# A graph kernel's rounds: rows of 133 edges with five self-loops taken out, and the loops added per chunk

## The chip, the cores and the metric

The kernel runs on one core of a Trainium2 chip. The metric is the device time of one execution in microseconds (us): the median of 10 runs is 10170.87 us, between 10168.81 and 10172.67. The engines go by short names: PE is TensorE, DVE is VectorE, ACT is ScalarE, POOL is GpSimd and SP is SyncE. SP, ACT and POOL also issue DMAs; gathers by index are issued by POOL.

## The reference

Two graph layers on 20000 nodes with 256 features and 340000 edges. The edges are 160000 random pairs, taken in both directions, and one self-loop for each node; they are sorted by destination with a stable sort, so a node's own loop is the last of its edges. Every edge, a loop too, has a type from 0 to 7. The first layer is relational: each type has a weight matrix of its own, and it is applied twice.

```python
def _rgcn_layer(x, W, self_w, b, src, dst, edge_type, num_nodes):
    xW = jnp.einsum('ni,rio->rno', x, W)
    msg = xW[edge_type, src]
    agg = jax.ops.segment_sum(msg, dst, num_segments=num_nodes)
    return agg + x @ self_w + b
...
h = jax.nn.relu(_rgcn_layer(x, W1, self_w1, b1, src, dst, edge_type, N_NODES))
out = _rgcn_layer(h, W2, self_w2, b2, src, dst, edge_type, N_NODES)
...
x = _layernorm(x + out)
```

The second layer is an attention over the same edges with 4 heads, in which source and destination are exchanged (it sums over all edges of equal source), followed by another layer norm. Everything is float32.

## The kernel before

The kernel has three stages: round one and round two (the two applications of the relational layer, `round_one` and `round_two`, both through `by_chunks`), and `attention`. A last branch recomputes everything in a general way if a flag (`bad`) says that an assumption about the edges does not hold.

**Tiles and chunks.** The sorted edges are cut into tiles of 128 (2657 of them, `COLS`); 16 tiles (`T`) make a chunk, of which there are 166 (`NC`; the last one has 17 tiles). The destinations of a chunk lie in a frame of 128 nodes that begins at `bases[j]`; those of tile t lie in a fixed window of that frame (`windows`), 16 to 19 nodes wide. All chunks are unrolled.

**What a tile does.** POOL gathers the 128 source rows (`gather`, L643). In the first 28 chunks of round one (`RAW`) a row is x in f32, later it is the row split into three bf16 parts (table `xs` in round one, `h2s` in round two). DVE makes one-hot matrices over (node in the window, type) from a code of each edge (`compare_raw`, L656; `compare`, L666). PE multiplies the gathered rows with the one-hots and adds up in PSUM (L764): for each of two halves of the features, for each part, for each half of the frame (64 nodes x 8 types, one PSUM bank of 512 columns) that the window touches. So a tile is 6 products in bf16, 12 where its window crosses the middle, and each streams 8 times as many columns as the window has nodes. Four banks hold the sums of the two feature halves (h) and the two frame halves (q).

**What a chunk does.** After tile 8 the first half of the frame is copied out of PSUM, after the last tile the second one (`evacuate`; three copies on ACT at L688, one on DVE at L686). The frame's first 12 nodes get what the chunk before left for them (L776). `make` then turns the frame's own rows (L695 or L698, copy `ot` on ACT at L701), multiplies them with the self weights (L707), adds the bias (L709) and multiplies the 8 types' sums with their weights, 16 products in f32 (L711); it yields between them, and one step of it runs after each tile of the next chunk. `use` finishes the rows and writes them to DRAM: `h2s` in round one; in round two a layer norm, a product with the attention's weights (L945, L953) and the tables for attention.

**Order of the work.** Instructions are emitted by hand in this order (`manual_schedule`): for each tile u, the gather of tile u + 23 (`AHEAD`; there are 24 buffers `g`), the comparisons, the tile's products, evacuation, one step of `make`, perhaps one step of side work, and one step of `use`. Each engine executes its share in that order. Side work comes from generators: `heads` (the rest of `edges`, then `fill_rows` and `ends_weights`), then `split_rows` (x into three bf16 parts, table `xs`), then `order`, which sorts the edges by source for attention (`rank` on ACT and DVE, `places`, `write` with the products L1271 on PE and the activations `two` on ACT, and `unpack`). In round one a tile takes a side step always until `rank` begins, then 2 tiles of 3, and 5 of 9 once `placed`; in round two 5 of 9. What is left over of `order` runs after round two; `unpack` has 23 gathers (L1361).

**The head.** `edges` reads source, destination and type in 5 slices of up to 5 x 128 tiles, 128 edges to a partition row, turns them on PE to 128 edges to a column, and makes of them the gather's index (`idx`), the code, and what the ordering needs (`hi`, `lo`, `kb`, `flat`). The index of slice 0 depends on the source's load alone. `load_ends` and `place_frames` compute `bases` from the first, middle and last edge of each chunk.

Of the kernel before, what the change touches and what calls it, by code (L numbers as in the profile page):

```python
# [47 lines left out]
P = 128  # L48
# [7 lines left out]
T = 16  # L56
CH = T * P
T3 = 17

TH = T // 2  # L60
BN = P // 2

HOME = BN - 1
CARRY = 12

AHEAD = 23

QS = 5

LOT = 3  # L70
# [7 lines left out]
def gnn_kernel(  # L78
# [37 lines left out]
    NC = E // CH  # L116

    RAW = min(28, NC // 2)
    COLS = -(-E // P)
    CS = QS * P  # L120
    assert CS % T == 0
    WORDS = NB * (T3 + 1)
    assert WORDS >= COLS
    assert COLS - NC * T in (0, 1)
# [6 lines left out]
    G = P // RG  # L131
    NK = -(-NB // 3)
    assert NB * 171 >> 9 == NB // 3 and NK <= STEP and NK * APART < 2 ** 23
    NQ = -(-COLS // P)
# [3 lines left out]
    slope = N * P / E  # L138
    vary = 3.0 * slope / P ** 0.5
    lows = [max(0, int(HOME + slope * (t - TH) - 3 - 0.35 * vary * abs(t - TH) ** 0.5)) for t in range(T + 1)]  # L140
    ends = [min(P, int(HOME + slope * (t + 1 - TH) + 4.5 + 0.5 * vary * abs(t + 1 - TH) ** 0.5)) for t in range(T)] + [P]
    lows[0], ends[T - 1] = 0, P
# [3 lines left out]
    halves = [(0, TH), (TH, T), (T, T + 1)]  # L146
    widths = [max(b - a for a, b in windows[f:g]) for f, g in halves]
    WIDE = max(P, NB, R * max(widths))
# [22 lines left out]

    slotd = dram.tile([EP, F], I32, name="slotd")
# [198 lines left out]
    def load_ends(pool, fb):  # L371

        ends_of = [pool.tile([1, NC], I32, name=f"ends{i}") if i != 1 else fb[0:1].bitcast(I32) for i in range(3)]
        for i, c in enumerate((0, CH // 2, CH - 1)):
            e = nc.scalar if i == 1 else nc.sync
            e.dma_start(ends_of[i], dst[:NC * CH].rearrange("(j c) -> c j", c=CH)[c:c + 1, :])
        return ends_of

    def place_frames(ends_of, to):
# [4 lines left out]
        nc.vector.tensor_single_scalar(mid, mid, HOME, op=ALU.subtract)  # L384
# [8 lines left out]
    def edges(k, keep, pool, ps, words):  # L393


        full, more = E // P, E % P or P
        if more == P:
            full -= 1
        QF, RF = full // P, full % P
        assert NQ == QF + 1  # L400
        slices = [(q, min(QS, NQ - q)) for q in range(0, NQ, QS)]

        def flat(of, q, n, none, e, after=0):

            c = pool.tile([P, QS, P], I32, name="flat", bufs=4)
            a = min(n, QF - q)
            of = of[after:]
            if a < n:
                nc.vector.memset(c[:, a:n], none)
            if a:  # L410
                e.dma_start(c[:, :a], of[q * P * P:(q + a) * P * P].rearrange("(q r p) -> r q p", r=P, p=P))
            if a < n:
                if RF:
                    e.dma_start(c[:RF, a], of[QF * P * P:full * P].rearrange("(r p) -> r p", p=P))
                if more > after:
                    e.dma_start(c[RF:RF + 1, a, :more - after], of[full * P:].unsqueeze(0))
            return c

        def number(c, n, e):
            f = pool.tile([P, QS, P], F32, name="flatf", bufs=3)  # L420
            e(f[:, :n], c[:, :n])
            return f

        def turned(f, q, n, to, idx=None):

            for i in range(0, n, 4):
                pt = ps.tile([P, 512], F32, name=("pr", "pl")[i // 4 % 2])
                m = min(4, n - i)
                for x in range(m):
                    w = min(P, COLS - (q + i + x) * P)  # L430
                    o = pt[:, x * P:x * P + w]
                    if f.dtype == BF16:
                        nc.tensor.matmul(o, f[:w, i + x, :], identb[:w, :w], start=True, stop=True)
                    else:
                        nc.tensor.transpose(o, f[:w, i + x, :], ident[:w, :w])
                w = min(m * P, COLS - (q + i) * P)
                if idx is not None:
                    nc.vector.tensor_scalar_max(idx[:, i * P:i * P + w], pt[:, :w], 0.0)
                nc.scalar.copy(to[:, i * P:i * P + w], pt[:, :w])
                yield  # L440

        for name, of in zip(("hi", "lo"), words):
            k[name] = of[:, :COLS]
        k["kb"] = keep.tile([P, COLS], FP16, name="kb")
        k["flat"] = keep.tile([P, NQ, P], F32, name="flatv")
        k["idx"], k["code"] = [], []
# [3 lines left out]
        begin = pool.tile([P, T + 1], F32, name="begin")  # L450
        end = pool.tile([P, T + 1], F32, name="end")
        for t, (a, b) in enumerate(windows):
            nc.gpsimd.memset(begin[:, t:t + 1], float(R * a))
            nc.gpsimd.memset(end[:, t:t + 1], float(R * (b - a)))
        q, n = slices[0]
        got = {0: [flat(src, q, n, -P, nc.sync), flat(dst, q, n, -NP, nc.sync), flat(etype, q, n, 0, nc.scalar)]}
        fb = pool.tile([P, NC], F32, name="fb")
        ends_of = load_ends(pool, fb)
        got[0].append(flat(dst, q, n, NP, nc.scalar, 1))
        odd = pool.tile([P, CS], BF16, name="odd")  # L460
        nc.vector.memset(odd, 0.0)
        own = pool.tile([P, CS], BF16, name="ownloops")
        nc.vector.memset(own, 0.0)

        def loads(s):
            return [flat(src, *slices[s], -P, nc.sync), flat(dst, *slices[s], -NP, nc.sync),
                    flat(etype, *slices[s], 0, nc.sync)]

        for s, (q, n) in enumerate(slices):
            fs, fd, ft, after = got.pop(s)  # L470
            c = q * P
            w = min(n * P, COLS - c)
            j = c // T
            m = (min(c + w, NC * T) - c) // T
            rest = w - m * T
            lo, hi = k["lo"][:, c:c + w], k["hi"][:, c:c + w]
            idx = keep.tile([P, w], I32, name=f"idx{s}")
            k["idx"].append(idx)
            block = pool.tile([P, QS, P], I32, name="block", bufs=1)
            if s:  # L480
                nc.vector.tensor_single_scalar(block[:, :n], fs[:, :n], 7, op=ALU.arith_shift_right)
            raw = fs
            fs = number(fs, n, nc.vector.tensor_copy)
            yield from turned(fs, q, n, lo, idx) if s else ()
            if not s:
                for _ in turned(fs, q, n, lo, idx):
                    pass
            fd = number(fd, n, nc.scalar.copy)
            if s:
                yield  # L490
                yield from turned(fd, q, n, hi)
            else:
                for _ in turned(fd, q, n, hi):
                    pass
            ft = number(ft, n, nc.scalar.copy)
            ct = pool.tile([P, CS], BF16, name="ct")
            if s:
                yield
                yield from turned(ft, q, n, ct)
            else:  # L500
                for _ in turned(ft, q, n, ct):
                    pass
                firsts = place_frames(ends_of, k["bases"])
                step = pool.tile([1, 2, NC], F32, name="step")
                ff = step[:, 1]
                nc.vector.tensor_copy(ff, k["bases"])
# [1522 lines left out]
```

## Time and profile before

| what | value |
|---|---|
| median of 10 runs | 10170.87 us |
| the profiled execution | 10177.42 us |
| its span, first to last instruction | 10175.6 us |
| mean granted TensorE clock | 0.957 |
| busy PE / PEld / DVE / ACT / POOL, us | 8655.1 / 6511.3 / 6451.5 / 6353.0 / 7659.7 |
| gathers of round one, first and last start | 7.2 and 3371.9 us |
| gathers of round two, first and last start | 3393.2 and 6720.4 us |
| gathers of attention, first start | 6754.3 us |

Busy time by stage, from the view of busy time by window:

| window, us | PE | DVE | ACT | POOL | clock |
|---|---|---|---|---|---|
| 0 to 590 | 497.9 | 334.6 | 201.1 | 445.1 | 0.96 |
| 590 to 2000 | 1203.0 | 680.5 | 683.1 | 1066.7 | 0.93 |
| 2000 to 3380 | 1210.7 | 719.1 | 644.0 | 1041.6 | 0.95 |
| 3380 to 6200 | 2603.4 | 1478.6 | 1652.3 | 2123.3 | 0.98 |
| 6200 to 6720 | 487.3 | 239.8 | 239.6 | 393.6 | 0.99 |
| 6720 to 10176 | 2652.9 | 2998.9 | 2932.9 | 2589.4 | 0.95 |

In the lines of the profile, L764 is line 764 of the kernel before; `g<-h2s,idx` is a gather that writes g from table h2s by the index; "x2657" counts instructions; then come busy time and the mean length of one, and behind the bar the idle time of the engine ahead of them, with what ended it. PEld is the loading of PE's stationary operand. Products overlap in PE's pipeline, so their lengths are longer than the distance from one start to the next. In the timeline a line has start, length, engine, line, operation, operands and count, and in brackets how long the engine was idle before and who ended that.

### The profile page before, as it was taken

The numbers are of one execution on the slowest core, as the hardware profiler recorded it, in microseconds if no ns is written. First come the engines' busy times: TensorE is split into PE (matmuls) and PEld (weight loads), VectorE is DVE, ScalarE is ACT, GpSimd is POOL, SyncE is SP. The second block draws the span as 40 slices with busy tenths as digits, with TensorE's granted clock in tenths as the row PEclk, the third lists the DMA queues.
The fourth block names the chain that finished last, engine by engine and source line by source line (L and its number), as shares of the span: only waits on it lengthen the run. The fifth ranks groups of instructions, "written<-read, shape, count | busy, mean of one in ns | idle before, by whom it ended". The sixth has DMA issues, their size and how long they took to land. (4 is left out here: it accounts for less than half of the span.)

```text
span 10175.6 us, 197290 instructions
## 1 busy us (share of the span) xinstructions
PE 8655.1 (85%) x67798; PEld 6511.3 (64%) x67798; DVE 6451.5 (63%) x14086; ACT 6353.0 (62%) x18671; POOL 7659.7 (75%) x8045
## 2 busy tenths in 40 slices
PE   8988888888898899999999999977777777777777
PEld 7866667666777777777777777754444444444444
DVE  6532366665444455555555555458888888888888
ACT  2466533332555555555555555538888888888888
POOL 7777777777777677777777777777777777777776
PEclk9999999999999999999999999989999999999999
DMA  5866666665666666666666666655555555555554
GB/s 168 255 204 177 177 178 177 178 178 171 177 179 179 180 189 188 190 189 188 189 188 189 189 189 189 190 157 155 155 154 152 155 155 155 153 154 155 153 154 129
DMA packets 860686, 1776.34 MB, mean 175 GB/s; under 512 B 196943, under 2 KB 526356, under 8 KB 859652
## 3 DMA queue, kind: packets, MB, share of 16 engines
q0 software_dynamic: 461200, 1384.74, 48.7%
q1 hardware_dynamic: 390620, 371.69, 11.5%
q8 instruction: 534, 8.75, 0.3%
q10 hardware_dynamic: 7848, 7.20, 0.2%
q14 instruction: 484, 3.96, 0.1%
HBM read 1629.85 MB, written 133.22 MB: 173 GB/s over the span
## 5 line engine op out<-in xcount | busy, mean ns | idle before, releaser
L764 PE MATMUL a<-s,g 128*128 128x152 bf16 (+9 forms) x34860 | 2870.0, 226 | 418.9 <-DMA g<-xs,idx 322.7
L1453 POOL DMA_INDIRECT g<-table3s,words x2657 | 2566.6, 966 | 813.5 <-issue 780.4
L643 POOL DMA_INDIRECT g<-h2s,idx x2657 | 2517.9, 948 | 830.6 <-issue 372.1
L711 PE MATMUL pm<-wt,to 128*128 128x256 f32 x10624 | 2921.5, 398 | 0.0
L764 PEld LDWEIGHTS <-g 128*128 128x128 bf16 x32844 | 2182.0, 99 | 949.2 <-DMA g<-xs,idx 420.5
L643 POOL DMA_INDIRECT g<-xs,idx x2209 | 2108.3, 954 | 680.6 <-issue 341.2
L1555 ACT ACTIVATE g<-g 128x64 f32<-128x64 f32 x8088 | 1993.1, 332 | 0.0
L711 PEld LDWEIGHTS pm<-wt,to 128*128 128x128 f32 x10624 | 1832.6, 192 | 187.9 <-issue 10.4
L1569 PE MATMUL po<-g,s 128*128 128x260 f32 x5314 | 1737.7, 418 | 96.3 <-DVE g L1561 70.6
L1513 DVE CUSTOM_DVE_ANT_0 dump<-pr,pen 128x768 bf16<-128x768 f32 x1876 | 1619.5, 907 | 30.0 <-PE pr L1510 28.6
L688 ACT COPY to<-a 128x512 f32<-128x512 f32 x996 | 545.1, 582 | 1376.6 <-PE a L764 1355.0
L1510 PE MATMUL pr<-hpt,pick 128*128 128x512 bf16 (+2 forms) x3752 | 936.6, 332 | 421.8 <-DVE top L1513 420.0
L1251 ACT ACTIVATE two<-b,words 128x157 f16<-128x157 f16 x2657 | 1120.6, 422 | 62.8 <-PE pl L1271 51.7
L1569 PEld LDWEIGHTS po<-g,s 128*128 128x128 f32 x5314 | 849.3, 196 | 454.5 <-ACT g L1546 78.3
L1252 ACT ACTIVATE two<-b,words 128x157 f16<-128x157 f16 x2657 | 1104.9, 416 | 0.0
L1510 PEld LDWEIGHTS <-pick 128*128 128x128 bf16 x3752 | 379.7, 101 | 922.3 <-issue 799.4
L776 DVE TENSOR_TENSOR to<-to,to 128x192 f32<-128x192 f32 x330 | 118.9, 360 | 1306.8 <-ACT to L688 1306.8
L666 DVE TENSOR_TENSOR s<-pi,code 128x1216 bf16<-128x1216 f32 x610 | 856.7, 1408 | 1.1 <-PE a L764 1.1
L1271 PE MATMUL pl<-two,a 128*128 128x314 f16 x2657 | 569.6, 303 | 122.4 <-ACT two L1252 118.3
L1013 DVE TENSOR_TENSOR b<-pi,kb 128x471 f16<-128x471 f32 (+1 forms) x896 | 567.9, 634 | 0.0
L1499 ACT CAST hpt<-pr 12x768 bf16<-12x768 f32 (+1 forms) x469 | 350.2, 747 | 344.1 <-PE pr L1497 343.9
L643 POOL DMA_INDIRECT g<-in_x,idx x448 | 440.5, 983 | 138.0 <-issue 67.7
(329 smaller groups left out, 8945.3 us busy)
## 6 DMA issues: line engine op xcount, KB each, us to landing
ob<-ownd SPq DMA_DIRECT2D x625, 128.0 KB
g<-h2s,idx POOLq DMA_INDIRECT x2657
g<-table3s,words POOLq DMA_INDIRECT x2657
g<-xs,idx POOLq DMA_INDIRECT x2209
h2s<-h SPq DMA_DIRECT2D x166, 192.0 KB
own<-h2s SPq DMA_DIRECT2D x166, 192.0 KB
xs<-xs SPq DMA_DIRECT2D x156, 192.0 KB
own<-xs SPq DMA_DIRECT2D x136, 192.0 KB
```

Source lines behind the costliest of these rows:

```text
L643: nc.gpsimd.indirect_dma_start(out=g, out_offset=None, in_=of, in_offset=bass.IndirectOffsetOnAxis(ap=idx[u // CS][:, u % CS:u % CS + 1], ...
L666: nc.vector.tensor_tensor(s, pi[:, :w].unsqueeze(1).to_broadcast([P, e - f, w]), codes(c, e - f).unsqueeze(2).to_broadcast([P, e - f, w]), ...
L711: nc.tensor.matmul(p, to[:, i % 2, i // 2, :P], wt[:, i % 2, i // 2, :], start=False, stop=(i == 2 * R - 1))
L764: nc.tensor.matmul(a[h, q][:, b:e, :].rearrange("p n r -> p (n r)"), g[:, v * D + h * P:v * D + (h + 1) * P], s, start=((h, q) not in begu ...
L1251: nc.scalar.activation(two[:, 0, :], made[m][:, x, :], AF.Copy, scale=k["hi"][:, c:c + 1])
L1252: nc.scalar.activation(two[:, 1, :], made[m][:, x, :], AF.Copy, scale=k["lo"][:, c:c + 1])
L1271: nc.tensor.matmul(pl[0].rearrange("p a b -> p (a b)"), a[:, x, :], ranked.pop((m, x)).rearrange("p a b -> p (a b)"), start=(first and x = ...
L1453: nc.gpsimd.indirect_dma_start(out=g[:, t, :], out_offset=None, in_=table3s, in_offset=bass.IndirectOffsetOnAxis(ap=to3[:, b, t:t + 1], ax ...
L1510: nc.tensor.matmul(pr[:, t:t + n, :], pick[:, h, :], k["hpt"][:, q + t:q + t + n, :], start=True, stop=True)
L1513: nc.vector.tensor_tensor_reduce(out=dump[:, :m, :].rearrange("p t e -> p (t e)"), in0=pr[:, :m, :].rearrange("p t e -> p (t e)"), in1=k[" ...
L1555: nc.scalar.activation(gh[:, h, :], gh[:, h, :], AF.Copy, scale=k["g"][:, t, D + h:D + h + 1])
L1569: nc.tensor.matmul(k["po"], k["s"][:, t, :] if t < n else ident, k["g"][:, t, :SR], start=(t == 0), stop=(t == n))
```

## The change

A row now has 133 edges (`LEN`) instead of 128. Of each row the self-loops among the nodes 0 to 4 after the row's first one, five of them, are taken out; the other 128 edges are pressed together and make a tile. There are 2557 tiles, 15 to a chunk, and 171 chunks (the last has 7 tiles). 120 rows make a block, and slices are two blocks wide. The 75 loops of a chunk are kept apart, with their nodes in the frame and their types; a round trip through DRAM (`loopd`) brings them from rows to columns.

- Index and code of a slice are made by more steps on DVE, with masks and predicated copies; the index now also depends on `bases`.
- For each chunk DVE makes two one-hots of its loops (`loop_marks`, at tile 6 of the chunk before); PE multiplies them to a mask of node and type, and DVE spreads that mask over a half of 64 nodes by 8 types (`loop_hots`, at tile 9).
- At tile 0 (first half of the frame) and at tile 3 (second half) PE multiplies the frame's own rows, 64 of them, with the spread mask (`loop_sums`). These products open the PSUM sums; no product of a tile does any more.
- Windows are 17 to 21 nodes wide instead of 16 to 19; the last tile's extra window is gone. `AHEAD` goes from 23 to 21, `RAW` from 28 to 30 chunks; in round one loop products are in f32 for 32 chunks.
- The side work changes its order: after two slices come `fill_rows` and `split_rows`, then the other slices. Its pace goes from 2 of 3 to 3 of 4 tiles, and from 5 of 9 to 3 of 5. `records` goes away, since `edges` makes `hi` and `lo` itself.

```diff
-T = 16
-CH = T * P
+T = 15
+LEN = P + 5
+DROP = LEN - P
+ROWS = 8 * T
+SLOTS = T * DROP
+CH = T * LEN
...
-AHEAD = 23
-
-QS = 5
+AHEAD = 21
+
+QS = 2
...
-    RAW = min(28, NC // 2)
...
+    RAW = min(30, NC // 2)
...
+            nc.vector.tensor_mul(same, same, over)
+            drop = pool.tile([P, QS, LEN], BF16, name="drop")[z, :n]
+            nc.vector.scalar_tensor_tensor(drop, far, DROP - 0.5, same, op0=ALU.is_lt, op1=ALU.mult)
...
+            nc.vector.tensor_scalar_min(by, far, float(DROP))
+            nc.vector.scalar_tensor_tensor(by, drop, -16.0, by, op0=ALU.mult, op1=ALU.add)
...
+            for x in range(DROP + 1):
...
+                mask = pool.tile([P, QS, P], BF16, name="mask", bufs=2)[z, :n]
+                nc.vector.tensor_single_scalar(mask, by[:, :, x:x + P], float(x), op=ALU.is_equal)
+                nc.vector.copy_predicated(kept, mask.bitcast(I16), v[:, :, x:x + P])
...
+            pt = turned(kept, q, n)
+            vt = pool.tile([P, QS * ROWS], I32, name="vt")[:, :w]
+            nc.scalar.copy(vt, pt)
...
+            nc.vector.tensor_single_scalar(k["idx"][:, c:c + w], vt, 9, op=ALU.arith_shift_right)
...
+            lot = loopd[q * ROWS * DROP:(q + n) * ROWS * DROP]
+            nc.sync.dma_start(lot.rearrange("(q r k) o -> r q (k o)", r=ROWS, k=DROP), loops)
...
+            nc.sync.dma_start(ls, lot.rearrange("(j s) o -> s (j o)", s=SLOTS))
...
+        def loop_marks(j):
...
+            a = sp.tile([SLOTS, P], BF16, name="la")
+            nc.vector.tensor_tensor(a, pi[:SLOTS, :P], k["node"][:, j:j + 1].to_broadcast([SLOTS, P]), op=ALU.is_equal)
+            b = sp.tile([SLOTS, R], BF16, name="lb")
+            nc.vector.tensor_tensor(b, pi[:SLOTS, :R], k["type"][:, j:j + 1].to_broadcast([SLOTS, R]), op=ALU.is_equal)
+            loop[j] = a, b
...
+        def loop_hots(j):
...
+            a, b = loop.pop(j)
+            x = WIDE + 1 + 3 * NK + j % 2 * R
+            po = pi[:, x:x + R]
+            nc.tensor.matmul(po, a, b, start=True, stop=True, skip_group_check=True)
+            s = sp.tile([P, 2 * BN * R], BF16, name="lm", bufs=1)
+            s = s.bitcast(F32) if raw and j < raw + 2 else s[:, :BN * R]
+            loop[j] = s
+            nc.vector.tensor_tensor(s.rearrange("p (n r) -> p n r", r=R), k["half"].unsqueeze(2).to_broadcast([P, BN, R]),
+                                    po.unsqueeze(1).to_broadcast([P, BN, R]), op=ALU.mult)
...
+        def loop_sums(j, q):
+
+            own, s = loaded[j][0], loop[j]
+            x = slice(q * BN, (q + 1) * BN)
+            n_parts = 1 if own.dtype == F32 else 3
+            for h in range(2):
+                a[h, q] = ps.tile([P, BN, R], F32, name=f"a{h}{q}")
+                for v in range(n_parts):
+                    nc.tensor.matmul(a[h, q].rearrange("p n r -> p (n r)"), own[x, v * D + h * P:v * D + (h + 1) * P],
+                                     s[x], start=(v == 0), stop=(v == n_parts - 1), skip_group_check=True)
...
+        while "ready" not in k:
+            next(side)
+        loop_marks(0)
+        loop_hots(0)
...
+            if t == TH - 2:
+                loop_marks(j + 1)
...
+            if t == TH + 1:
+                loop_hots(j + 1)
+            if t in (0, 3):
+                loop_sums(j, t // 3)
...
-                                         start=((h, q) not in begun), stop=(v == n_parts - 1), skip_group_check=True)
-                        begun.add((h, q))
+                                         start=False, stop=(v == n_parts - 1), skip_group_check=True)
...
+        for i, _ in enumerate(parts):
+            yield
+            if i % 2:
+                yield
+        with tc.tile_pool(name="edges", bufs=1) as cp:
+            pools[0] = cp
+            yield from rest
...
-                  lambda u: not ranks.begun or (u % 9 < 5 if ranks.placed else u % 3), False, ranks, RAW, parts)
+                  lambda u: not ranks.begun or (u % 5 < 3 if ranks.placed else u % 4), False, ranks, RAW, parts)
```

## The prediction

> **What bounds the kernel now.** I read the page first: the 40 slices and the costliest groups.
>
> ```profile
> PE   8988888888898899999999999977777777777777
> ...
> POOL 7777777777777677777777777777777777777776
> ...
> L711 PE MATMUL pm<-wt,to 128*128 128x256 f32 x10624 | 2921.5, 398 | 0.0
> ...
> L643 POOL DMA_INDIRECT g<-h2s,idx x2657 | 2517.9, 948 | 830.6 <-issue 372.1 <-PE a L764 231.3 <-PE pl L1271 90.8
> ```
>
> The two rounds fill slices 1 to 26, attention the rest. POOL shows 7 throughout and looks far from full; PE shows 8 in round one and 9 in round two. Which of them sets the pace? The timeline of POOL in round two answers for the gathers:
>
> ```profile
> 5002.18 0.95 POOL L643 DMA_INDIRECT g<-h2s,idx  x1 [0.30 <-PE a L764]
> 5003.43 0.95 POOL L643 DMA_INDIRECT g<-h2s,idx  x1 [0.30 <-PE a L764]
> 5004.69 0.95 POOL L643 DMA_INDIRECT g<-h2s,idx  x1 [0.31 <-PE pl L1271]
> ```
>
> A gather starts every 1.25 us, and the gap is 0.30 us whoever is named as its releaser, "issue" included: POOL never waits longer there, it is simply full at 0.95 + 0.30. So a tile costs POOL 1.25 us and a chunk of 16 tiles 20.0 us. Next, the waits of PE's weight loads and matmuls: first round one from 800 to 2000 us, then round two from 3500 to 6200 us (us in total, times, longest):
>
> ```profile
> PEld L764 <- DMA g<-xs,idx: 225.5, 230, 3.5
> ...
> PEld L764 <- DMA g<-h2s,idx: 11.0, 20, 0.9
> ...
> PE pl L1271 <- ACT two L1252: 85.0, 230, 0.6
> PE pr L1304 <- DVE here L1293: 74.2, 22, 5.9
> ```
>
> In round one PE waits for gathers 225 us in 1200. In round two almost never: there PE is as slow as POOL. To see how near, I counted in the timeline how long after the end of the u-th gather the u-th tile's first product starts:
>
> | tile | 90 | 210 | 450 | 540 | 2400 | 3000 | 3600 | 4200 | 4700 | 5300 |
> |---|---|---|---|---|---|---|---|---|---|---|
> | lag, us | 20.7 | 4.3 | 19.8 | 5.7 | 2.2 | 11.2 | 17.0 | 23.6 | 26.0 | 2.3 |
>
> (Tiles from 2657 on are round two.) While round two carries the ordering's products (L1271), the lag climbs to 26 us, which is all 23 gathers of AHEAD. **PE needs about 20.2 us a chunk there, 0.15 more than POOL, and is the bound already**; buffers hide it. Where it catches up, it shows its own speed: tiles 90 to 210 in 137.9 us, 18.4 us a chunk (raw, f32 products); tiles 450 to 540 in 99.2 us, 17.6 a chunk, of which 1.5 are waits for ACT (ot, L701) behind the copies of the row split.
>
> **What the change does to each.** Prices are start to start, from PE's timeline:
>
> ```profile
> 3379.04 7.17 PE L711 MATMUL pm<-wt,to 128*128 128x256 f32 x32
> 3386.05 0.70 PE L1271 MATMUL pl<-two,a 128*128 128x314 f16 x4
> ...
> 5011.20 1.35 PE L764 MATMUL a<-s,g 128*128 128x152 bf16 x18
> 5012.38 0.56 PE L1271 MATMUL pl<-two,a 128*128 128x314 f16 x3
> ...
> 7503.06 0.48 PE L1510 MATMUL pr<-hpt,pick 128*128 128x512 bf16 x2
> 7503.38 0.60 PE L1569 MATMUL po<-g,s 128*128 128x260 f32 x2
> ```
>
> 18 products of 152 columns take 1.18 us: 0.43 ns a column. The L1510 pair is one product of 512 and one of 256 columns: 0.32 us for 768, so 0.21 us for 512. An f32 product is two records; 32 records of 256 columns take 7.01 us, 0.219 each, so an f32 product of 512 columns costs 4 x 0.219 = 0.88 us. 128 active rows or 1 active column make no visible difference in the rows; the columns streamed do.
>
> *Removed.* 100 tiles a round (2657 to 2557): 200 gathers x 1.25 = 250 us of POOL. A chunk falls to 15 tiles, 18.8 us of POOL.
>
> *Added on PE, per chunk.* loop_sums: 2 halves x 2 feature halves x 3 bf16 parts = 12 products of 512 columns, 12 x 0.215 = 2.58 us. While own rows come in f32 (32 chunks): 4 x 0.88 = 3.5 us. loop_hots: one product of 8 columns, under 0.05. Windows widen: their sum is 285 nodes over 16 tiles before, 296 over 15 after, so a chunk streams 296 x 8 x 6 columns instead of 285 x 8 x 6: 528 x 0.43 = +0.23 us. The make (32 L711 records and the rest) stays the same per chunk, and there are 171 chunks instead of 166, which the sums below include. Net +2.83 us a chunk (+3.8 raw) against 1.25 us less time on POOL.
>
> *Where that lies.* PE is in order, and loop_sums stands in its stream at tiles 0 and 3. Its operands are early: own rows are loaded two chunks ahead, the marks are made at tiles 6 to 9 of the chunk before; its PSUM was evacuated at tile 8 and at the last tile, about 4 us before tile 3 needs it. So I give it no wait, but no cover either: nothing hides 2.8 us on an engine that is the bound.
>
> *DVE and ACT.* loop_marks and loop_hots add three DVE instructions, about 0.3 + 0.2 + 0.7 us (nearest rows: L1258, 384 wide, 0.55; L686, 512 wide, 0.69). DVE is busy 1479 of 2820 us in round two; covered. If that cover went, 1.2 us a chunk would be 400 us. The edge slices' DVE steps (266 instead of 640 wide, more of them) run beside gathers as before. SP gets 11 stores and 11 loads of loops and five more chunks' rows; it is not near full. The row split moves ahead of the later slices, with its 157 loads and 157 stores on SP and two ACT copies each; that removes POOL's 7.8 us wait for xs, worth nothing once PE is the bound.
>
> *Head.* Now the first gather starts at 7.2 us and the first product at 19.9. After, the index needs the frames (ends landed at 7.9, then 8 small DVE instructions and nine tiny products), some 15 DVE instructions of 266 columns at about 0.35 (640-wide ones take 0.49 to 0.82), twelve masks and predicated copies at 0.3, a turn and two copies: first gather about 24 us. The first chunk also waits for the loops: 16 more instructions and reductions, a store and a load through DRAM (the first load here is issued at 0.8 and used at 4.2 us), marks: first product about 46 us. POOL loses 17 us, PE 26.
>
> **The sum, along PE.** In the built program's order the ordering's products span chunks 137 to 331 of 342 (123 to 322 of 332 before).
> - raw, 32 chunks: 18.4 + 3.8 = 22.2 us, 710
> - chunks 32 to 136, 105: 17.6 - 1.5 (split done earlier) + 2.8 = 18.9; POOL asks 18.8; with friction 19.2: 2016
> - 34 chunks of round one with L1271: 18.9 + 13.3 x 0.133 + waits for "two" 0.5 = 21.2: 721
> - 22 us between rounds, as now
> - round two, 160 chunks: 20.2 + 2.8 = 23.0 if every wait stays. The idle of PE before L1271 and L1304 is 159 us over 134 chunks, 1.2 us each; longer PE time gives ACT and DVE more room, so I take half of it as hidden: 22.4, 3584
> - 11 chunks without L1271: 19.9, 219
>
> 46 + 710 + 2016 + 721 + 22 + 3584 + 219 = 7318 us, where round two now ends at 6722: +596. The 23 gathers of unpack (29 us on POOL after round two) fall into PE's backlog: -25. Attention (3450 us) is untouched. The profiled execution took 10177.4 us (span 10175.6), so 10748; the median of the runs is 6.5 us below the profiled one: **about 10740 us, 5.6% slower**.
>
> **The Trainium skill.** "TensorE: Matmul & The Clock Gate", section "Why this matters for your kernels", says that a matmul of few contraction rows takes as long as a full one and gains only from tiles running side by side. The half-row loop products stand three tiles apart in the stream, so by it nothing is saved; no row here has 64 rows. The same page's "Back-to-back issue gap" gives 131 ns for sustained 512-column matmuls; the 0.215 us above differ, and the measurement decides. By its figure 3720 products would cost 312 us less, and the time would be about 10430.
>
> **Rivals.**
> 1. *POOL stays the pace* (faster). If half-row products cost little, under about 0.05 us, and PE's waits melt, the time is 10171 - 250 + 17 = about 9940. For it: PE's busy time holds pipelined tails. Against: at the prices above, without any wait or tail, PE's products of round two sum to 17.4 us a chunk now (L764 5.9, L711 7.0, L1271 1.8, L707 and L953 0.9 each, L945 0.4, L698 0.3, L709 0.2), so 20.2 after, over POOL's 18.8. 4%.
> 2. *All friction melts.* PE at bare prices: 32 x 20.4, 105 x 18.8, 34 x 18.9, 160 x 20.2, 11 x 18.8 make 6776 with head and gap: 10171 + 54 - 25 = 10200. Between this and 10430 I give 10%, and 2% to ending within 0.2% (about what a measurement of this kernel can tell from no change).
> 3. *New waits on top*: products on half the rows break the pipeline on entry and exit, twice a chunk, and tile 3 waits for DVE's evacuation when DVE is late. A product of 152 columns lasts 0.235 us in the trace at a spacing of 0.066, so a drain is worth some 0.17 us; four make 0.7, x 342 = 230 more, and a wait of 0.3 another 100: 10970 to 11070. Above 11050: 6%.
> 4. *The fallback runs*: the masks take the wrong edges, or a window is too narrow, and the general path follows, a second whole computation, thousands of us. On the reference's inputs every full row of 133 holds five loops among its first five nodes and no edge leaves its window. Under 1%.
>
> **Numbers.** Forecast 10430 to 11050, 78%: low end, about half of all friction gone (the five stages at 21.2, 18.8, 20.2, 21.2 and 19: 10432); high end, every wait kept and some added (22.6, 20.5, 22, 23.2, 20.5: 11053). Chances: faster 4%, same 2%, slower 94%. "TensorEngine Tiling", section "Key Properties", says that a change of tiling mode drains the engine; no run here shows it yet.
>
> **What would show it.** Right: in round two POOL's gap before L783 is no longer 0.30 but waits for PE's release of g, a chunk takes 22 to 23 us, L843's bf16 products start 0.21 us apart, PE waits for no gather. Wrong: gathers still every 1.25 us in round two, or L843 much cheaper; then rival 1. First gather at 24 us and first product at 46 test the head.

## The result and the profile after

The changed kernel takes 10716.47 us (median of 8 runs, 10711.81 to 10726.24) beside 10170.4 us for the kernel before in the same series: **1.0538 times as long, 95% interval 1.0529 to 1.0547**. The forecast was 10740. The profiled execution took 10727.29 us with a span of 10725.6, where the kernel before had a span of 10175.6: 550 us more.

One thing has to be known to read the runs: the first eight experiments below (x and y) ran on two chips on which the kernel before takes 13628 us, the last four (z) on one on which it takes 10184; so the first eight are compared with the kernel before on their own chip only.

Where the 550 us are, from the starts of the first L707 (after: L884) product of a chunk in the trace:

| stage | before | after | difference |
|---|---|---|---|
| up to the make of chunk 0 | 44.4 | 77.8 | +33 |
| the next 32 chunks (raw, f32; before, the last 4 in bf16) | 658.0 | 785.1 | +127 |
| rest of round one and the gap | 2718.4 | 2715.1 | -3 |
| round two | 3304.4 | 3706.0 | +402 |
| from there to attention's first gather | 29.0 | 27.1 | -2 |
| attention | 3421.3 | 3414.5 | -7 |

A chunk holds 15 tiles in place of 16, so the two columns do not count the same chunks. In round two 165 distances of 20.0 us have become 170 of 21.8: some 290 us because a chunk takes longer, and some 110 because there are five more chunks, each with all its products besides those of the tiles.

The page of the changed kernel, its slices and costliest groups:

```profile
PE   8988999999999999999999999997777777777777
...
POOL 6655777777767666666666666666777777777776
...
L783 POOL DMA_INDIRECT g<-h2s,idx x2557 | 2417.9, 946 | 1330.3 <-PE a L952 956.0
...
L888 PE MATMUL pm<-wt,to 128*128 128x256 f32 x10944 | 2970.6, 394 | 0.0
...
L843 PE MATMUL a<-lm,own 64*128 64x512 bf16 (+1 forms) x3976 | 1060.3, 400 | 2.1 <-DVE lm L832 1.6
```

L783 is the old L643, L888 the old L711 and L952 the old L764; L843 has the new loop products. POOL's digit in round two is now 6, PE's is 9 throughout, and the group of gathers has 1330 us of idle time before it where it had 831, of which PE's products over g ended 956. In the timeline of POOL at the place shown before:

```profile
5007.52 0.94 POOL L783 DMA_INDIRECT g<-h2s,idx  x1 [1.47 <-PE a L952]
5008.84 0.94 POOL L783 DMA_INDIRECT g<-h2s,idx  x1 [0.37 <-PE a L952]
5010.66 0.94 POOL L783 DMA_INDIRECT g<-h2s,idx  x1 [0.87 <-PE a L952]
5012.02 0.94 POOL L783 DMA_INDIRECT g<-h2s,idx  x1 [0.42 <-PE a L952]
```

The gap is no longer the fixed 0.30 us but the wait for PE to let go of a buffer. The gather takes 0.94 us as before; only the gaps have become irregular, with one releaser. PE's waits in the same stretch of round two, from 3700 to 6700 us (total, times, longest, us):

```profile
PE pr L1481 <- DVE here L1470: 48.7, 18, 3.4
PE pl L1448 <- ACT two L1429: 13.2, 61, 0.3
```

No gather is among them. L1448 is the old L1271 and L1481 the old L1304. L1271's wait for ACT was 85 us in 2700 us of round two before; L1448's is 13 in these 3000.

### The profile page after: what moved, and what is told of

Same layout as the page of the kernel before. It is cut to its first block, busy times and chain, and to the rows that moved or that the text cites. A ratio compares the mean times of both kernels' runs of the same rounds, so it can differ in the third digit from the quotient of the medians.

```text
span 10725.6 us, 206363 instructions
## 1 busy us (share of the span) xinstructions
PE 9650.2 (90%) x71367; PEld 6923.4 (65%) x71367; DVE 7006.4 (65%) x15947; ACT 6512.1 (61%) x19127; POOL 7452.1 (69%) x7843
## 4 chain that ended last, share of the span: by engine, by line
PE 63%; DVE 14%; issue 7%; ACT 7%; POOL 7%; DMA 3%; SPq 0%; ACTq 0%; DVEq 0%; POOLq 0%
PE pm L888 23%; PE a L952 20%; PE a L843 9%; POOL g L1630 7%; DVE dump L1690 6%; PE pm L884 3%; PE pl L1448 3%; ACT g L1732 3%; DVE g L1738 2%; DMA g<-table3s,words 1%; PE pr L1147 1%; ACT hpt L1676 1%; PE pm L875 1%; PE po L1746 1%; PE pm L886 1%
## 5 line engine op out<-in xcount | busy, mean ns | idle before, releaser
L783 POOL DMA_INDIRECT g<-h2s,idx x2557 | 2417.9, 946 | 1330.3 <-PE a L952 956.0
L888 PE MATMUL pm<-wt,to 128*128 128x256 f32 x10944 | 2970.6, 394 | 0.0
L952 PE MATMUL a<-s,g 128*128 128x160 bf16 (+10 forms) x33744 | 2954.2, 230 | 6.3 <-DVE s L797 2.5
L952 PEld LDWEIGHTS <-g 128*128 128x128 bf16 x31704 | 2154.0, 98 | 708.7 <-issue 271.1
L783 POOL DMA_INDIRECT g<-xs,idx x2107 | 2004.2, 951 | 772.5 <-PE a L952 377.0
L888 PEld LDWEIGHTS pm<-wt,to 128*128 128x128 f32 x10944 | 1877.7, 191 | 186.8 <-issue 2.5
L1428 ACT ACTIVATE two<-b,words 128x157 f16<-128x157 f16 x2557 | 1079.6, 422 | 89.9 <-DVE b L1207 58.5
L843 PE MATMUL a<-lm,own 64*128 64x512 bf16 (+1 forms) x3976 | 1060.3, 400 | 2.1 <-DVE lm L832 1.6
L1429 ACT ACTIVATE two<-b,words 128x157 f16<-128x157 f16 x2557 | 1061.3, 415 | 0.0
L808 DVE TENSOR_TENSOR s<-pi,code 128x1176 bf16<-128x1176 f32 (+1 forms) x622 | 906.7, 1458 | 0.0
L340 DVE CAST row<-row 128x4 bf16<-128x4 f32 x171 | 29.5, 173 | 1026.5 <-ACT row L1149 1026.5
L783 POOL DMA_INDIRECT g<-in_x,idx x450 | 443.6, 986 | 276.1 <-PE a L952 194.1
L843 PEld LDWEIGHTS <-own 64*128 64x128 bf16 x3720 | 305.2, 95 | 412.4 <-issue 61.8
```

Of the source, the lines that this page charges most:

```text
L783: nc.gpsimd.indirect_dma_start(out=g, out_offset=None, in_=of, in_offset=bass.IndirectOffsetOnAxis(ap=idx[:, u:u + 1], axis=0))
L808: nc.vector.tensor_tensor(s[:, :m], pi[:, 1:w + 1].unsqueeze(1).to_broadcast([P, m, w]), codes(c, m).unsqueeze(2).to_broadcast([P, m, w]), ...
L843: nc.tensor.matmul(a[h, q].rearrange("p n r -> p (n r)"), own[x, v * D + h * P:v * D + (h + 1) * P], s[x], start=(v == 0), stop=(v == n_pa ...
L888: nc.tensor.matmul(p, to[:, i % 2, i // 2, :P], wt[:, i % 2, i // 2, :], start=False, stop=(i == 2 * R - 1))
L952: nc.tensor.matmul(a[h, q][:, b:e, :].rearrange("p n r -> p (n r)"), g[:, v * D + h * P:v * D + (h + 1) * P], s, start=False, stop=(v == n ...
L1428: nc.scalar.activation(two[:, 0, :], made[m][:, x, :], AF.Copy, scale=k["hi"][:, c:c + 1])
```

## The experiments

Line numbers differ by up to 5 from those of the changed kernel where an edit adds lines. "Per chunk" is from the same starts as in the table. z2 is compared with the kernel before, whose lines it shifts by 3. There were twelve runs, in two groups.

### On the chips of 13628 us

The changed kernel itself was not run on these chips, so no run here gives an edit's worth against it; each ratio is against the kernel before.

**x1 and y1, no loop products** (the same kernel twice; the loops are added in the last chunk of a round alone, and elsewhere a tile's first product opens the sum):

```diff
-            if t in (0, 3):
+            if t in (0, 3) and j == NC - 1:
                 loop_sums(j, t // 3)
...
```

> The changed kernel without its loop products (loop_sums stays in the last chunk alone; the loops' terms are left out of the result), marks and spread mask still made. Theory, PE's in-order stream sets the time wherever it needs over 18.8 us a chunk: round two falls from 22.0 to about 19.4 us a chunk (160 x 2.6 = 416 us), round one's chunks with the ordering's products from 20.7 to 18.8 (65), the first 32 from 24.1 to 20.3 (122), the edge stage by 20, the middle not at all, since POOL paces it: about 10090 us. Rival, the other parts (longer head, DVE's edge steps, wider windows, marks) carry most of the 546 us: no lower than 10450.

> The first look at this edit was on a chip where the kernel before took 13628 us; this is the same kernel again, which leaves the loop products out (all but those of the last chunk), so loops are not added to the sums. Beside a kernel before of about 10171 us. Theory (the products stand bare on PE, which is the bound): round two goes from 22.0 us a chunk to about 19.3, where POOL's 18.8 is near, so -430; the ordering's chunks of round one -45, raw chunks 3.5 x 32 = -110; the middle of round one is paced by POOL and stays: about 10130 us. Rival (the loss is elsewhere: head, turns of the edge slices, longer chunks): at least 10450 us. If the chip is again a slow one, only the ratio counts: below 0.998 for the theory, above 1.03 for the rival.

Measured: x1 13531.24 us beside 13627.73, ratio 0.9937 [0.9920, 0.9954]; y1 13536.49 beside 13629.12, ratio 0.9932 [0.9912, 0.9951]. The sign is the theory's, and y1's bound for it (below 0.998) holds; the size is not tested, because here round two takes 23.6 us a chunk even without the products.

**x3, every loop product twice** (so each loop is added twice):

```diff
-                for v in range(n_parts):
+                for v in range(2 * n_parts):
+                    c = v % n_parts * D + h * P
...
```

> The changed kernel with each loop product done twice (the result counts the loops twice). Theory: another 2.6 us a chunk in round two (445 us in 171 chunks), in round one's chunks with the ordering (90), 3.8 in the first 32 (122), and now in the middle too, where PE stands at POOL's 18.8 and would go to about 21.3 (some 210): about 11570 us. Rival, the loops cost by what their position waits for or drains rather than by columns streamed: the second set adds less than half of the first, below 11000.

Measured: 13970.31 us, ratio 1.0251 [1.0233, 1.0268]. Against x1 on the same chip, without the products, that is 439 us for two sets of them, far less than the theory has on a chip of 10171 us, and nearer to the rival in size; one set cannot be told from the other here, and why so little of PE's time shows in the total stays open. In PE's timeline a block of 12 products takes 2.69 us, a block of 6 takes 1.40 in the changed kernel: the second set costs PE 0.215 us a product.

**x4 and y4, all loop products at tile 5, the two row halves alternating** (the same kernel twice):

```diff
-            if t in (0, 3):
-                loop_sums(j, t // 3)
+            if t == 5:
+                loop_sums(j)
...
+            for h, v, q in [(h, v, q) for h in range(2) for v in range(n_parts) for q in range(2)]:
...
```

> The changed kernel with all loop products at tile 5, the lower and the upper half of the own rows taking turns, so that neighbours use different rows of the array and different PSUM banks; same result. Theory with overlap of half-row products: a pair takes one product's 0.215 us, 1.3 us a chunk saved, in the first 32 about 1.9: 160 x 1.3 + 34 x 1.3 + 32 x 1.9 + 20 = 330 us less, about 10390. Without overlap: 10716 within 30.

> The loop products of a chunk stand together at tile 5, and those of the upper and of the lower 64 rows alternate. If two products on different row halves run side by side on TensorE, 12 of them take 6 x 0.216 = 1.3 us in place of 2.6: round two about -1.2 x 160 = -190, raw -1.7 x 32 = -55, the ordering's part -35: about 10430 us. If they run one after another, 10716 within 30 us. If a switch between row halves drains the engine, longer: 12 x 0.1 us x 342 = +400.

Measured: x4 13688.05 us, ratio 1.0051 [1.0034, 1.0067]; y4 13670.92, ratio 1.0029 [1.0017, 1.0041]. The totals say little here, but the starts in PE's timeline are clear: the two products of a pair start 3 ns apart, the next pair 212 ns later, and the 12 together take 1.40 us, as long as 6 of one half take by themselves. Products on different halves of the rows do run side by side, and y4's third case, a drain at every switch of halves, is out.

**x5, all at tile 5, but one half after the other:**

```diff
-            for h, v, q in [(h, v, q) for h in range(2) for v in range(n_parts) for q in range(2)]:
+            for h, v, q in [(h, v, q) for q in range(2) for h in range(2) for v in range(n_parts)]:
```

> The same products at tile 5, but the lower half's first and then the upper half's, so that products of different rows meet once. It takes away the wait for PSUM that the upper half could have at tile 3. Theory, place and waits cost nothing: 10716 within 30. Rival, the wait for evacuation at tile 3 is part of the loss: 100 us less or more.

Measured: 13737.11 us, ratio 1.0082 [1.0065, 1.0099]; the total decides between neither case. In PE's timeline the block takes 1.85 us:

```profile
5017.51 1.92 PE L843 MATMUL a<-lm,own 64*128 64x512 bf16 x12
5019.36 0.57 PE L953 MATMUL a<-s,g 128*128 128x152 bf16 x6
```

So some overlap comes without alternating: of the 12 starts, four come 8 to 19 ns behind the one before.

**y2, the loop products alone, put into the kernel before** (with a mask of zeros, so they add nothing):

```diff
-AHEAD = 23
+AHEAD = 21
...
+            if t in (0, 3):
+                zero_sums(j, t // 3)
```

> The kernel before with the change's loop products alone: 12 half-row products of 512 columns (4 in f32) at tiles 0 and 3 of every chunk, with a mask of zeros, so they add nothing; AHEAD is 21 for room. Theory (the products are the loss; the 200 gathers saved are worth nothing in round two and only something where POOL sets the pace): round two 20.2 + 1.9 = 22.1 us a chunk, 160 chunks, +300; the ordering's chunks of round one +1.9 x 30 = +57; raw +3.5 x 32 = +110; the middle of round one, where POOL asks 20.0 and PE has room of 1.5, +1 x 100 = +100 at most: 10171 + 470 = about 10640 us. Rival (the gathers saved gave back much, the products cost more than the whole loss): 10800 to 10960 us. Second rival (products on half the rows are nearly free): within 30 us of 10171.

Measured: 13807.53 us, ratio 1.0131 [1.0110, 1.0153]. In PE's timeline a block of 6 takes 1.39 us from start to next start (6005.07 to 6006.46), as long as in the changed kernel, so the products are not nearly free on PE, as the second rival has it. Between the other two these chips do not decide. `AHEAD` was changed along and not tested by itself, so not all of the 1.3% need be the products'.

**y8, the later edge slices turn their tiles later:**

```diff
+            for _ in range(5 if s else 0):
+                yield
             pt = turned(kept, q, n)
...
+            for _ in range(4 if s else 0):
+                yield
```

> The later edge slices turn their kept and rec tiles on PE some steps later (five and four more pauses in the order of work), when DVE and ACT have made them. Theory: the roughly 8 us that PE waits at each turn of the ten later slices go, and with them the slow products after the wait: -60 to -90 us, 10625 to 10655 us. Rival (PE then waits at the gathers or at the next turn instead, the stage is bound by DVE): 10716 within 20 us.

Measured: 13655.46 us, ratio 1.0016 [1.0006, 1.0026]. In its trace the first 30 raw chunks take 23.0 us each, where x4, y4 and x5 need 25.0 to 25.4: 60 to 70 us, the theory's size. y1, without loop products, needs 25.4 too, so the loops are not what these chunks wait for here.

### On a chip of 10184 us

**z0, the changed kernel unaltered:**

> The changed kernel itself, unaltered, as the base for the other kernels on such chips. On chips where the kernel before takes 13629 us, the like kernel with all loop products at tile 5 took 13737 (1.008); its block of 12 products takes 1.85 us in PE's timeline, the two blocks of the changed kernel 2 x 1.40 with their ends, so the changed kernel takes up to 0.95 us a chunk longer where PE sets the pace: 13737 to 13900 us, 1.008 to 1.02. If the excess of 1.054 were the same on every chip: 14365 us. On a chip where the kernel before takes 10171 us: 10716.

Measured: 10736.5 us beside 10184.15, ratio 1.0539 [1.0524, 1.0553], the excess of the result again (1.0538).

**z1 and z2, every second gather left out, in the changed kernel and in the kernel before:**

```diff
         def gather(u):
+            if u % 2:
+                got[u] = got[u - 1]
+                return
```

> Leaves out every second gather; the products of the odd tiles read the tile before, so the sums are of other rows. POOL asks 9.4 us a chunk in place of 18.8, so PE alone sets the pace of the rounds. Theory for a chip where the kernel before takes 10171 us (round two is bound by PE): 21.5 to 22.0 us a chunk in round two as with all gathers (21.9 to 22.1), total 10630 to 10716; rival (POOL is the pace): under 20. Theory for a chip with 13629 us (the other engines get their instructions late while gathers run): round two falls from 24.4 to under 22.5; rival (the slowness has nothing to do with the gathers): 24.4 within 0.5.

> The kernel before with every second gather left out (the odd tiles read the tile before, so the sums are of other rows). PE alone sets its pace. Theory (PE was the bound of round two by friction, not by POOL): 19.0 to 20.2 us a chunk in round two, 2.0 to 2.9 less than the changed kernel with half its gathers. Rival (POOL was the pace, PE had room): under 18.5, 3.5 or more below the changed kernel with half its gathers. If half-row products were free, the two kernels would be within 0.5 us a chunk.

Measured: z1 10706.16 us, ratio 1.0515 [1.0499, 1.0531], 30 us less than z0; z2 9663.02 us, ratio 0.9489 [0.9475, 0.9504], 521 us less than the kernel before. z1 and z2 lie where the theory had them, 10630 to 10716 us and 19.0 to 20.2 us a chunk in round two. By stage, us per chunk:

| stage | before | z2 | after | z1 |
|---|---|---|---|---|
| middle of round one (chunks 50 to 100) | 20.11 | 15.81 | 18.69 | 18.63 |
| round two (chunks 2 to 156 or 160) | 20.14 | 20.14 | 21.99 | 21.98 |

This is the run that settles most. POOL's waits, 3000 to 6000 us of z2:

```profile
POOL g L646 <- PE a L767: 1702.6, 901, 7.9
```

And PE's in the same stretch:

```profile
PE pl L1274 <- ACT two L1255: 94.8, 256, 0.6
PE pr L1307 <- DVE here L1296: 83.5, 24, 5.9
```

POOL waits for PE for more than half of the time, half of its work is gone, and round two does not move by 0.1 us a chunk: **PE, with its small waits for ACT and DVE in the ordering, was the bound of round two in the kernel before too, and the gathers that the change saves are worth nothing there.** It was a near thing: the gathers alone ask 16 x 1.25 = 20.0 us a chunk, and with half of them all of round two is 16 us shorter (3288.3 us in place of 3304.4). Where it falls by 4.3 us, in the middle of round one, POOL was the pace. In the changed kernel taking gathers away moves neither stage. z2's 15.81 against z1's 18.63 is PE without and with the loops (and the wider windows): 2.8 us a chunk. In round two the expected 2.0 to 2.9 between z1 and z2 came out as 1.84, just below. A run of the changed kernel without its loop products, on a chip like this one, is missing; that they are the loss rests on z1, z2, z3 and the timeline.

**z3, alternating halves and late turns together** (the edits of x4 and y8):

> Both edits that helped together: the loop products of both row halves alternate at tile 5 (12 of them take 1.40 us in PE's timeline, as 6 do one after another), and the later edge slices turn their tiles some steps later. On a chip with 13629 us for the kernel before, the first alone gave 13671 and the second 13655; if they add up, 13560 to 13620, below the kernel before. On a chip with 10171: PE saves 1.4 us a chunk and two changes of mode, some 0.2 each: round two 21.9 to 20.2, 10716 - 270 - 60 - 60 = about 10320, still above the kernel before.

Measured: 10431.33 us, ratio 1.0240 [1.0226, 1.0254]; 305 us less than z0, and 111 more than expected on such a chip. A chunk's block in PE's timeline of z3:

```profile
5000.68 1.47 PE L847 MATMUL a<-lm,own 64*128 64x512 bf16 x12
5002.08 0.57 PE L957 MATMUL a<-s,g 128*128 128x152 bf16 x6
```

And one of the two blocks of the changed kernel:

```profile
5015.55 1.47 PE L952 MATMUL a<-s,g 128*128 128x168 bf16 x18
5016.95 1.47 PE L843 MATMUL a<-lm,own 64*128 64x512 bf16 x6
5018.35 0.53 PE L952 MATMUL a<-s,g 128*128 128x136 bf16 x6
```

The same 1.40 us from start to next start, for 12 products and for 6. Bare, that frees 1.49 us a chunk (one block and two changes between full and half rows). Round two fell from 21.99 to 20.92, by 1.07: PE's idle time rose from 68 to 136 us in 3000, 0.45 us a chunk, so some of the waits for ACT that the loops had covered came back (those of the ordering's products, from 13 to 65 us). Expected was 20.2. The raw chunks fell by 2.5 us each, to 22.2. No version here that does all of the work beats the kernel before.

## Why the prediction was right

**PE is the bound of round two, POOL has no room to give.** Right, and shown by z2 and z1. The figure was 20.2 us for PE; z2 gives 20.14. It was read off the lag of PE behind the gathers, and not off busy shares.

**The loop products stand bare on PE.** Right. Forecast 0.215 us each; the trace has 216 ns from start to start, on 64 rows as on 128. The third rival's drain exists, too, but is smaller than its 0.17 us. From starts in round two: going in, a 168-column product takes 168 ns where it otherwise takes 73, and a 128-column f32 record 205 for 109, so 95; going out, the last loop product takes 308 for 216, so 92. The sum had no price for these changes. Four changes make 0.4 us a chunk, and the loops cost 2 x (1.40 + 0.095) = 2.99 us where the sum had 2.58. The Trainium skill, "TensorEngine Tiling (Array Packing)", section "Key Properties", says that a change of tiling mode drains the engine; the trace agrees, with 0.09 us for each change. The rule that the prediction took from "TensorE: Matmul & The Clock Gate" (nothing is gained by few rows, unless tiles run side by side) agrees in both halves, 216 ns and 3 ns. Its 131 ns for sustained 512-column products is not what this kernel has. The 215.7 ns that its section "Wait — 56ns, not 53.3ns?" gives for 512 columns back to back is.

**Friction.** Right in kind, too small in size. Forecast was that half of 1.2 us is hidden, 0.6. Spacings by their medians sum to 2324 us of 2700 in round two before, 17.4 us a chunk (as the rivals' sum had it), and to 2793 of 3000 after, the changes of mode included, 20.5. What is not bare fell from 2.8 to 1.5 us: bare PE rose by 3.1 and the chunk by 1.85 only. PE's idle time, 192 us in those 2700 and 68 in the 3000, is 0.9 us a chunk of that; the rest stays open. z3 shows the reverse.

**The sum, term by term:**

| term, us | forecast | measured |
|---|---|---|
| first gather / first product | 24 / 46 | 24.3 / 51.8 |
| raw, 32 chunks | 710 | 785 |
| middle of round one, 105 chunks | 2016 | 2002 |
| 34 chunks of round one with the ordering, and the gap | 721 + 22 | 713 |
| round two, 160 chunks | 3584 | 3518 |
| the remaining 11 chunks (10 at the end, and the first up to its make) | 219 | 214 |
| unpack hidden | -25 | -2 |
| attention | 0 | -7 |

The forecast's list puts the 34 chunks in round two; its count is that of round one. The total was 0.2% off because the raw stage (+75) and unpack (+23) went against round two (-66) and the ordering (-30): that it came so near is luck.

*The middle* came out right on a figure that was off: PE was put at 17.6 less 1.5 us there, 16.1; z2 has 15.8. With the loops, the wider windows and a tile less, PE needs what POOL needs, 18.6 (z1) and 18.8.

*Raw* is the step that failed. It took the edge slices' DVE steps to "run beside gathers as before" and gave their turns on PE no price. In PE's stream the turn of a slice (L446) waits for DVE and ACT, and everything behind it waits too. PE's timeline of the changed kernel at one of them:

```profile
877.77 1.47 PE L843 MATMUL a<-lm,own 64*128 64x512 bf16 x6
...
889.33 0.66 PE L446 MATMUL pr<-ident,kept 120*128 120x120 f32 x2 [8.45 <-ACT kept L683]
889.93 2.74 PE L843 MATMUL a<-lm,own 64*128 64x512 bf16 x6
...
893.37 2.00 PE L884 MATMUL pm<-wt,ot 128*128 128x256 f32 x4
```

8.45 us of waiting, and then the same 6 products take twice as long: they start 0.40 to 0.43 us apart in place of 0.216, the L884 records 0.43, until some 8 us after the restart. The view of busy time by window (PE, PEld, DVE, ACT, POOL, then PE's granted clock) shows it as a clock:

```profile
520.00:760.00 240.00, 216.53 (x1114) 172.29 (x1115) 174.31 (x496) 43.50 (x106) 138.07 (x140) 0.95 0.38 102
760.00:1000.00 240.00, 187.28 (x1374) 137.57 (x1373) 142.62 (x395) 47.58 (x107) 124.08 (x129) 0.83 0.47 129
1000.00:1240.00 240.00, 240.00 (x2088) 186.31 (x2085) 71.52 (x119) 165.58 (x303) 181.81 (x192) 1.00 0.62 179
```

0.83 in the window with the turns, 1.00 in the next. The Trainium skill, "TensorE: Matmul & The Clock Gate", section "Why this matters for your kernels", warns of idle gaps over about 3 us for this reason; here a gap of 8.45 us did it. The raw stage as a whole, in the kernel before, the changed kernel and z3:

```profile
44.00:702.00 658.00, 574.74 (x3825) 509.70 (x3823) 334.84 (x711) 274.39 (x610) 495.38 (x510) 0.96 0.70 212
78.00:863.00 785.00, 717.29 (x3901) 569.12 (x3901) 514.07 (x1369) 226.83 (x588) 474.19 (x482) 0.95 0.59 173
71.00:781.00 710.00, 653.20 (x3882) 537.95 (x3882) 462.07 (x1198) 217.78 (x567) 469.84 (x482) 0.96 0.64 189
```

DVE's busy time grew from 335 to 514 us. In the changed kernel PE idles for 68 of the 785 us, 61 of them ahead of the turns, at L446 and L444; the two largest:

```profile
PE pr L446 <- ACT kept L683: 32.4, 8, 9.6
PE pr L446 <- DVE kept L564: 22.0, 6, 7.2
```

The price of 18.4 us came from a stretch (150 to 290 us of the kernel before) in which PE idles for 6 of 140 us, at a clock of 0.98. Idle time beyond that share (some 34 us) and the lower clock (some 24) make nearly 60 of the 75 us that the sum lacks; this is an estimate from these windows, and the rest stays open.

Turning later is not the whole cure. y8 puts it at 60 to 70 us on the slower chips. In z3 PE's waits for turns fall from 61 to 5 us, but waits for the one-hots that DVE makes come in their place:

```profile
PE pi L832 <- DVE s L801: 17.0, 16, 3.0
PE a L957 <- DVE s L801: 15.8, 7, 4.5
PE pi L832 <- DVE s L812: 10.0, 2, 8.1
```

PE still idles for 57 of 710 us. z3's raw stage is 81 us shorter than z0's (709.7 us, 791.1), but at the forecast's price pairing alone is worth half of 3.5 us in each of 32 chunks, 56 us. This points at the slices' steps on DVE, which stand ahead of turns and one-hots alike; no run tests them alone.

*Unpack* failed as well. Its 23 gathers did fall into PE's backlog (they start at 7250.6 us, while the last product over gathered rows ends at 7276), but there was next to nothing to hide. The kernel before, SP and POOL:

```profile
6749.02 0.34 SPq L960 DMA_DIRECT2D table3s<-row  x1
6749.16 0.94 POOL L1361 DMA_INDIRECT t<-recs,at  x1 [0.30 <-issue]
6754.32 0.99 POOL L1453 DMA_INDIRECT g<-table3s,words  x1 [4.23 <-DVE words L1381]
```

And the changed kernel:

```profile
7278.03 0.94 POOL L1538 DMA_INDIRECT t<-recs,at  x1 [0.30 <-DMA t<-recs,at]
7307.92 0.34 SPq L1154 DMA_DIRECT2D table3s<-row  x1
7311.04 0.94 POOL L1630 DMA_INDIRECT g<-table3s,words  x1 [32.07 <-DMA ownd<-uo]
```

Attention gathers from `table3s`, and the last chunk's rows are stored there 23.7 us after its first L707 product before, 24.0 us after its first L884 product now. Before, the unpack gathers (6721.6 to 6750.1 us) ran beside that finish already. With them out of the way the first gather follows the last store by 3.1 us in place of 5.3: that is the 2 us. z2 and z1 agree: their unpack gathers end 45 and 60 us ahead of attention's first one, and the stage still takes 27.0 and 27.2 us.

**The rivals.** POOL stays the pace: out in round two, by the half gathers. All friction melts: out, 1.5 us a chunk are left. New waits on top: its drain is there with 0.4 us in place of 0.7, and the wait of tile 3 is not (L843 has 2.1 us of idle time before it in all 3976 products).

## What to carry to other kernels

Before counting a saving on a busy engine, find in each stage which engine is late against which: here the lag of the consumer behind the gathers told, where busy shares of 7 and 9 tenths did not, and halving the gathers of the kernel before shows in one run that 100 fewer gathers are worth nothing in round two. Fewer edges to a chunk also mean more chunks, and each brings its fixed products: some 110 us of the 402 that round two grew by here. Work that moves from a queue that only feeds to the in-order engine that is the bound is paid in full, less what of that engine's own small waits it covers, and the waits come back when the work is made cheaper. Where half-row products cannot be avoided, keep both halves adjacent and alternate them: 12 then cost what 6 do, and a place in the stream saves two changes of mode of 0.09 us each. The chunk then fell by 1.07 us of the 1.49 that this freed.

## What the runs showed of the hardware that was not expected

**Two products on different row halves start 3 ns apart** when they alternate in the stream (x4, y4, z3), and still overlap in part when the halves follow one another (x5).

**PE's half speed lasts.** After a wait of 8.45 us PE ran at half speed for about 8 us (889.3 to 897.2), so this wait cost some 4 us beyond its length, an estimate from the doubled distances.

**Chips on which the same program takes a third longer.** On two chips the kernel before took 13628 us, steadily (13600 to 13653 in 26 runs), and attention, which no edit touches, about 5380 us (y4 5381, x5 5378) in place of 3415. An instruction takes its usual time (ACT's below 0.33 us in the median on both kinds of chip, a gather 0.95); the engines stand idle in between. ACT's timeline in attention on one of them (y4), like instructions ahead of which the profile shows no wait:

```profile
8993.89 2.74 ACT L1733 ACTIVATE g<-g 128x64 f32<-128x64 f32 x11
8996.99 0.35 ACT L1733 ACTIVATE g<-g 128x64 f32<-128x64 f32 x1 [0.36 <-issue]
8997.70 0.35 ACT L1733 ACTIVATE g<-g 128x64 f32<-128x64 f32 x1 [0.37 <-issue]
8999.11 0.35 ACT L1733 ACTIVATE g<-g 128x64 f32<-128x64 f32 x1 [1.05 <-issue]
8999.81 0.35 ACT L1733 ACTIVATE g<-g 128x64 f32<-128x64 f32 x1 [0.35 <-issue]
```

Eleven at 0.24 us, then one every 0.70 or 1.40. It was seen only while gathers are under way: of the pairs of such instructions in attention with more than 20 gather packets started within 1 us of the first one's start, 10.8% of 5498 start over 0.5 us apart; of 1932 with fewer packets, none; on the chip of the result, none of all 7430. In the same spell DVE idles for 3.19 and 6.74 us and PE for 3.23 and 6.04. So gathers may cost the other engines something on these chips, which would fit the small excess of x4, x5, y4 and y8 there, but a kernel with fewer gathers was not tried on them, and what holds the instructions up stays open.
